# In-place normalization of the next job's rows in the gate and up stage, and the half chunk's split moved from VectorE to GpSimd

## The chip, the cores and the metric

The kernel runs on one core of a Trainium2 chip. The metric is the device time of one execution in microseconds (us); the figure for a kernel is the median of its runs. Every time below comes from those runs or from one profiled execution.

## What is computed

2048 rows of 1024 values (two sequences of 1024) pass three layers, each added to its input: half a feed-forward net, a convolution along the row, and half the same feed-forward net again.

```python
x = x + 0.5 * ffn(layernorm(x))
x = x + attn(layernorm(x))          # a long convolution, its kernel from a state space model
x = x + 0.5 * ffn(layernorm(x))

def layernorm(x): return (x - mean(x)) / sqrt(var(x) + 1e-5)
def ffn(x):       return (silu(x @ Wg) * (x @ Wu)) @ Wd
# Wg, Wu: 1024 x 2752, Wd: 2752 x 1024, each 4 bits with a scale and a zero point per 128 rows
```

## The kernel before

**Jobs.** The rows are cut into four blocks of 512. A job is one block in one of the two feed-forward layers, so there are eight, in the order (block, layer) = (0,1) (1,1) (0,3) (1,3) (2,1) (3,1) (2,3) (3,3); they are called job 0 to job 7. Layer 2, the convolution, has no job of its own: for blocks that left layer 1, its pieces are hung into the gate and up stage of the following job (jobs 1, 2, 5 and 6).

**Two stages in a job.** The *gate and up stage* (`gate_up`, L716) walks 64 steps: eight waves of output chunks, eight groups of 128 input channels in each wave. Waves 0 to 4 (steps 0 to 39) hold six accumulators in PSUM, waves 5 and 6 (steps 40 to 55) four, the last wave (steps 56 to 63) five, the fifth for the *half chunk*: 2752 is 21 chunks of 128 and 64 more, and the last 64 gate and 64 up channels share one accumulator. In each step TensorE (PE in the profile) multiplies every chunk by the low and the high part of the activations (`xTl` in f16, `xTh` in fp32r, L742), and the accumulator is then multiplied in place by the ratio of two groups' scales (`scaled`, L710): on ScalarE (ACT, L712) for the gate chunks, on VectorE (DVE, L714) for the up chunks. The next step's matmul on that accumulator needs the scaled value. At a wave's end `gated` (L767) forms silu(gate) * up: ACT makes the silu `g` (L769), DVE the product `hf` (L772), and GpSimd (POOL) splits it into `hh` (a cast, L774) and `hl` (the rest, L776). `gated_half` (L779) does so for the half chunk, with `hf_half` on DVE (L786) and the split on DVE too:

```python
nc.vector.tensor_copy(both[high], hf[high])                                              # L788
nc.vector.tensor_tensor(both[low], hf[high], both[high].bitcast(F32), ALU.subtract)      # L789
```

The *down stage* (`down`, L794) walks 44 steps, two halves of 22 chunks. A step is eight matmuls (L805), `hl` and `hh` into four accumulators, and four scalings: two on ACT and two on DVE (L714). Chunk 21, the half chunk, is used in step 21 first.

**Weights.** POOL casts the byte weights of a step to fp32r (`make_weights`, L690) three steps before their use; the sync engine's DMA queue (SP) loads the bytes one step before that.

**The next job's activations.** While a job runs, the rows of the next job lie in four tiles `x` of 128x1024. Their moments (L187, L188) and inverse deviations (L210 to L213) are taken in the gate and up stage. For a next job in layer 1 (made in jobs 3 and 4), the moments are written at step 44 and the deviations at step 45. For a next job in layer 3 they follow the convolution, at steps 27 and 28, in job 1 at steps 61 and 62; there the tiles are also saved to DRAM (L1441). From job 1 on, `turn_by_dma` (L253) then does the rest in ten pieces for each of the four tiles t, hung at steps 2+9t and later of the down stage. The first piece normalizes the tile into a new tile `xn`, in two halves on DVE (L269). The next six are POOL's: `hi` and `top` (casts, L276, L277), `mid` (L279) and `lo` (L281), for each half. Then come three DMAs that transpose, and two POOL sums. A job loads its own rows again from DRAM at step 21 of its down stage, for the residual sum.

**What sets the order.** The kernel is written as one program with hooks: a function hung at a step is written ahead of that step's matmuls. A scheduler then orders each engine's instructions, and may put one ahead of others as soon as its inputs are expected to be ready. Where a hook is wrapped in `in_order_of_writing` (L141) with an engine's name, this engine's instructions keep the order in which they were written. Every engine runs its instructions strictly in order. Before the change, the pieces of `turn_by_dma` were so wrapped for POOL and SP, and not for DVE.

Of the kernel before, what the change touches and what calls it, by code (L numbers as in the profile page):

```python
# [9 lines left out]
F32 = mybir.dt.float32  # L10
# [8 lines left out]
ALU = mybir.AluOpType  # L19
AX = mybir.AxisListType  # L20
ET = mybir.EngineType
# [34 lines left out]
def macaron_s4_kernel(  # L56
# [31 lines left out]
    nc = tc.nc  # L88
# [41 lines left out]
    def t4(name):  # L130
        return xpool.tile([P, HID], F32, tag="x", name=name)
# [9 lines left out]
    def in_order_of_writing(f, *engines):  # L141

        start = len(nc.cur_bb.bb.instructions)
        got = f()
        written = list(nc.cur_bb.bb.instructions)
        for e in engines:
            last = next((i for i in reversed(written[:start]) if i.engine == e), None)
            for ins in written[start:]:
                if ins.engine == e:
                    if last is not None:  # L150
                        tc.add_manual_dep(
                            ins,
                            last.name,
                            mybir.DependencyInfo(
                                mybir.DependencyClass.NoSync, mybir.DependencyReason.DATA
                            ),
                            reason="order of writing",
                        )
                    last = ins
        return got  # L160


    x = {}
    ln = {}
# [59 lines left out]
    def turned(n, name):  # L224

        ps = bank(name)
        for k in range(4):
            nc.tensor.transpose(ps[:, bass.ts(k, P)], n[:, bass.ts(k, P)], ident)  # L228
        return ps.rearrange("p (c t) -> p c t", c=4)
# [4 lines left out]
    def turn(b, t, n, half, by_pool=False):  # L234
        k = ln[b, t][2]
        if b not in pieces:
            pieces[b] = [
                xtpool.tile([P, NC, TB], dt, tag=f"xT{w}", name=f"xT{w}_{b}_{k}")
                for w, dt in (("h", F32R), ("l", F16))
            ]  # L240
        hi, lo = (a[:, 4 * half : 4 * half + 4, bass.ts(t, P)] for a in pieces[b])
        ps = turned(n, f"pt_{b}_{k}_{t}_{half}")
        if by_pool:
            both = gpool.tile([P, TB], F32, tag="g", name=f"turn_{b}_{k}_{t}_{half}")
            both = both.rearrange("p (c t) -> p c t", c=4)
            nc.scalar.copy(both, ps)
            nc.gpsimd.tensor_copy(hi, both)
            nc.gpsimd.tensor_tensor(lo, both, hi.bitcast(F32), ALU.subtract)
        else:
            nc.scalar.copy(hi, ps)  # L250
            nc.vector.tensor_tensor(lo, ps, hi.bitcast(F32), ALU.subtract)

    def turn_by_dma(b, t, after):  # L253

        k = ln[b, t][2]
        name = f"{b}_{k}_{t}"
        if b not in pieces:
            pieces[b] = [  # L260
                xtpool.tile([P, NC, TB], dt, tag=f"xT{w}", name=f"xT{w}_{b}_{k}")
                for w, dt in (("h", F32R), ("l", F16))
            ]
        hi_t, lo_t = (a[:, :, bass.ts(t, P)] for a in pieces[b])
        halves = [slice(0, 512), slice(512, HID)]
        m, r, _ = ln[b, t]
        n = t4(f"xn_{name}")
        for own in halves:
            nc.vector.tensor_scalar(n[:, own], x[b][t][:, own], m, r, ALU.subtract, ALU.mult)  # L269
        yield  # L270
        hi = t4(f"hi_{name}").bitcast(F32R)
        top = hfpool.tile([P, HID], BF16, tag="hf", name=f"top_{name}")
        mid = hfpool.tile([P, HID], BF16, tag="hf", name=f"mid_{name}")
        lo = gpool.tile([P, HID], F16, tag="g", name=f"lo_{name}")
        for own in halves:
            nc.gpsimd.tensor_copy(hi[:, own], n[:, own])  # L276
            nc.gpsimd.tensor_copy(top[:, own], n[:, own])  # L277
            yield
            nc.gpsimd.tensor_tensor(mid[:, own], hi[:, own].bitcast(F32), top[:, own], ALU.subtract)  # L279
            yield  # L280
            nc.gpsimd.tensor_tensor(lo[:, own], n[:, own], hi[:, own].bitcast(F32), ALU.subtract)  # L281
            yield
        both = t4(f"turned_{name}").bitcast(BF16).rearrange("p (i c t) -> p i c t", i=2, c=NC)

        def transposes():
            nc.sync.dma_start(both[:, 0], top, transpose=True)
            nc.sync.dma_start(both[:, 1], mid, transpose=True)
            nc.sync.dma_start(lo_t, lo, transpose=True)

        transposes()  # L290

        def sums():
            for half in range(2):
                own = slice(4 * half, 4 * half + 4)
                nc.gpsimd.tensor_tensor(hi_t[:, own], both[:, 0, own], both[:, 1, own], ALU.add)  # L295
                yield

        after.append(sums())
# [273 lines left out]
    def split(w):  # L572
        raw, z = packed[w]
        even = t4(f"even_{w}").bitcast(I32)[:, : width_of(w)]
        return signed_bytes(w, raw, even, z)
# [203 lines left out]
    def gated_half(j, p):  # L779

        last = rat[:, 2 * WIDE, GK - 1 :]
        low, high = slice(0, HALF), slice(HALF, P)
        g = gpool.tile([P, TB], F32, tag="g", name=f"g_{j}_half")
        nc.scalar.activation(g[high], p[low], AF.Silu, scale=last[low])
        hf = hfpool.tile([P, TB], F32, tag="hf", name=f"hf_{j}_half")
        nc.vector.scalar_tensor_tensor(hf[high], p[high], last[high], g[high], ALU.mult, ALU.mult)  # L786
        both = hpool.tile([P, TB], F32R, tag="h", name=f"hb_{j}")
        nc.vector.tensor_copy(both[high], hf[high])  # L788
        nc.vector.tensor_tensor(both[low], hf[high], both[high].bitcast(F32), ALU.subtract)  # L789
        h[WIDE] = (both,)  # L790

    yT = {}

    def down(j, b, hooks):  # L794
# [605 lines left out]
    def fast():  # L1400
        for j, (b, k) in enumerate(JOBS):
            prev = JOBS[j - 1] if j else None
            after = JOBS[j + 1] if j + 1 < len(JOBS) else None
            up, dn = {}, {}

            def at(hooks, s, f):
                hooks.setdefault(s, []).append(f)

            if prev:
# [3 lines left out]
                if pk == 1:  # L1413
                    late = 34 if j == 1 else 0
# [51 lines left out]
            if j == 1:  # L1466
                tables = s4_tables()
                for i in range(S4_PIECES):
                    piece = lambda: in_order_of_writing(lambda: next(tables, None), ET.DVE)
# [3 lines left out]
            if after:  # L1473
                ab, ak = after
                if ak == 1:
                    at(up, 55 if j == 0 else 6, lambda: load_x(ab, rows_of(u, ab)))
                    if j == 0:
                        steps = [(dn, d) for d in range(3, 8)]
                        in_pieces(at, steps, lambda: moments_by_tile(ab, 1))
                        newton = lambda: deviations(ab, 1, LIFT)  # L1480
                        at(dn, 8, lambda: in_order_of_writing(newton, ET.DVE))
                    else:
                        both = lambda: moments(ab, 1)
                        at(up, 44, lambda: in_order_of_writing(both, ET.DVE))
                        at(up, 45, lambda: deviations(ab, 1, LIFT))
                an = {}

                pool = j == 0

                def anorm(t):  # L1490
                    an[t] = normalized(ab, t)

                o = 9 if j == 0 else 0
                turns = {}

                def turning(t):
                    if t not in turns:
                        turns[t] = [], []
                        turns[t] += (turn_by_dma(ab, t, turns[t][1]),)
                    rest = turns[t][1] or turns[t][2:]  # L1500
                    next(rest[0], None)

                for t in range(NT if j else 0):
                    late = (12, 13) if t == NT - 1 else (13, 17)
                    for d in (0, 1, 2, 3, 5, 6, 7, 9) + late:
                        piece = lambda t=t: turning(t)
                        piece = lambda piece=piece: in_order_of_writing(piece, ET.Pool, ET.SP)
                        at(dn, 2 + 9 * t + d, piece)
                for t in range(0 if j else NT):
                    at(dn, o + 1 + 4 * t, lambda t=t: anorm(t))  # L1510
                    at(dn, o + 2 + 4 * t, lambda t=t: turn(ab, t, an[t][:, :512], 0, by_pool=pool))
                    at(dn, o + 4 + 4 * t, lambda t=t: turn(ab, t, an[t][:, 512:], 1, by_pool=pool))
            o, gap = (27, 3) if j == 0 else (21, 4)
            at(dn, o, lambda: load_x(b, rows_of(u, b) if k == 1 else saved(b)))
            for t in range(NT):
# [3 lines left out]
        b = JOBS[-1][0]  # L1519
# [205 lines left out]
```

## Time and profile before

| | |
|---|---|
| median of three runs | 2126.0 us (2123.86 to 2126.82) |
| profiled execution | 2125.47 us |
| its span, first to last instruction | 2123.6 us |
| busy: PE, DVE, ACT, POOL | 98%, 80%, 66%, 61% of the span |
| granted TensorE clock | 0.996 |
| gate and up stage of jobs 2, 3, 7 | 187.4, 159.5, 157.6 us |
| down stage of jobs 2, 3, 7 | 83.8, 83.7 and 94.7 us (the last with the end of the program) |

A job begins about every 240 to 270 us. Job 2's gate and up stage runs from 572.3 to 759.7 us of the span and its down stage from 759.7 to 843.4 us, job 3's from 843.4 and from 1002.9 us; these two jobs are read most below. The timeline prints an instruction's start, its duration, engine, line and tiles, then in brackets the idle time of the engine before it and what ended that. Tile names stand without numbers. Matmuls overlap in the pipeline: in a full stretch one of 512 columns *starts* every 0.225 us in the gate and up stage and every 0.23 us in the down stage, whatever duration is printed, so a stall of PE is read from the distance of two starts.

### The profile page before, as it was taken

What the parts mean: (1) busy time and instruction counts of PE and PEld (TensorE: products, weight loads), DVE (VectorE), ACT (ScalarE), POOL (GpSimd) and SP (SyncE); (2) the same over time, 40 slices, a digit from 0 to 9 for tenths busy, and PEclk for the clock granted to TensorE, in tenths of its full rate; (3) what the DMA queues carried; (4) which work ended last, traced back from release to release, by engine and by line L of the source; (5) the groups of instructions that cost most, each with busy time, mean ns of one, the idle gap of its engine ahead of it and who ended that gap; (6) DMA issues with size and microseconds to landing.
All of it is one profiled execution on the core that took longest, in us unless ns stands there. A gap on an engine that the chain in (4) does not pass through costs nothing.

```text
span 2123.6 us, 30212 instructions
## 1 busy us (share of the span) xinstructions
PE 2071.9 (98%) x9556; PEld 1405.8 (66%) x9556; DVE 1688.6 (80%) x2757; ACT 1396.8 (66%) x2185; POOL 1290.1 (61%) x1678
## 2 busy tenths in 40 slices
PE   6999999999999999999999999999999999999997
PEld 3555675677776567665776567675676766866576
DVE  8988877778888787778877888877788787777776
ACT  5777777736655766676667766547665467667765
POOL 6877838647654577455855568455684546845541
PEclk9999999999999999999999999999999999999999
DMA  4434321113311125211441124111251111441111
GB/s 139 122 86 143 100 72 53 36 54 82 100 39 54 34 58 167 66 30 34 121 135 38 29 50 124 42 53 31 49 123 38 51 39 41 123 128 34 33 35 58
DMA packets 239143, 151.02 MB, mean 71 GB/s; under 512 B 98683, under 2 KB 226532, under 8 KB 238974
## 3 DMA queue, kind: packets, MB, share of 16 engines
q1 hardware_dynamic: 237958, 147.12, 24.6%
q8 instruction: 78, 1.28, 0.3%
q10 hardware_dynamic: 728, 1.29, 0.2%
q14 instruction: 91, 0.75, 0.1%
q0 software_dynamic: 288, 0.59, 0.1%
HBM read 104.45 MB, written 25.50 MB: 61 GB/s over the span
## 4 chain that ended last, share of the span: by engine, by line
PE 88%; DVE 8%; ACT 1%; DMA 1%; issue 1%; POOL 1%; SPq 0%; ACTq 0%; DVEq 0%; POOLq 0%
PE pg L742 56%; PE po L805 26%; PE pc L1131 3%; DVE po L714 2%; PE pb L827 1%; PE pb L1131 1%; DVE pg L714 1%; DVE xn L269 1%; PE st L228 1%; DVE hf L772 0%; DMA b<-wq 0%; DVE rawd L565 0%; POOL q L598 0%; DMA x<-in_L_attn_u_dram 0%; ACT g L769 0%
## 5 line engine op out<-in xcount | busy, mean ns | idle before, releaser
L712 ACT ACTIVATE pg<-pg,rat 128x512 f32<-128x512 f32 x1240 | 786.3, 660 | 423.6 <-PE pg L742 422.5
L714 DVE TENSOR_TENSOR pg<-pg,rat 128x512 f32<-128x512 f32 x1168 | 777.4, 693 | 179.8 <-PE pg L742 175.1
L742 PE MATMUL pg<-xTh,w_up 128*128 128x512 f32 x2752 | 851.0, 438 | 3.0 <-DVE pg L714 1.7
L742 PE MATMUL pg<-xTl,w_up 128*128 128x512 f16 x2752 | 722.0, 382 | 6.2 <-POOL xTl L1580 3.1
L690 POOL CAST w_up<-b 128x768 fp32r<-128x768 int8 (+2 forms) x490 | 376.3, 774 | 504.7 <-PE pg L742 406.6
L742 PEld LDWEIGHTS pg<-xTh,w_up 128*128 128x128 f32 x2752 | 519.7, 189 | 176.9 <-DVE pg L714 14.5
L712 ACT ACTIVATE po<-po,ratd 128x512 f32<-128x512 f32 x660 | 431.2, 661 | 189.9 <-PE po L805 189.8
L805 PE MATMUL po<-hl,w_down 128*128 128x512 f32 x1344 | 535.9, 402 | 14.8 <-DVE po L714 13.2
L805 PE MATMUL po<-hh,w_down 128*128 128x512 f32 x1344 | 521.6, 391 | 0.0
L714 DVE TENSOR_TENSOR po<-po,ratd 128x512 f32<-128x512 f32 x620 | 428.7, 697 | 102.7 <-PE po L805 97.6
L742 PEld LDWEIGHTS <-w_up 128*128 128x128 bf16 x2752 | 228.6, 99 | 330.6 <-issue 155.8
L690 POOL CAST w_down<-bd 128x512 fp32r<-128x512 int8 x352 | 224.3, 639 | 193.1 <-PE po L805 118.8
L805 PEld LDWEIGHTS po<-hl,w_down 128*128 128x128 f32 x1344 | 252.0, 188 | 102.8 <-DVE po L714 40.6
L805 PEld LDWEIGHTS po<-hh,w_down 128*128 128x128 f32 x1344 | 252.6, 188 | 47.0
L776 POOL TENSOR_TENSOR hl<-hf,hh 128x512 fp32r<-128x512 f32 x168 | 217.8, 1297 | 8.1
L772 DVE SCALAR_TENSOR_TENSOR hf<-pg,rat,g 128x512 f32<-128x512 f32 x168 | 123.1, 748 | 48.1 <-ACT g L769 40.8
L769 ACT ACTIVATE g<-pg,rat 128x512 f32<-128x512 f32 x168 | 110.7, 686 | 50.5 <-PE pg L742 34.3
L774 POOL CAST hh<-hf 128x512 fp32r<-128x512 f32 x168 | 105.6, 629 | 58.5 <-PE pg L742 31.0
L281 POOL TENSOR_TENSOR lo<-xn,hi 128x512 f16<-128x512 f32 x48 | 61.7, 1286 | 0.0
L187 DVE BATCH_NORM_STATS2 stats<-x 128x6 f32<-128x512 f32 x88 | 58.5, 676 | 0.5
L279 POOL TENSOR_TENSOR mid<-hi,top 128x512 bf16<-128x512 f32 x48 | 57.0, 1187 | 0.0
L295 POOL TENSOR_TENSOR xTh<-turned 128x512 fp32r<-128x512 bf16 x48 | 55.8, 1163 | 0.0
(214 smaller groups left out, 1116.0 us busy)
## 6 DMA issues: line engine op xcount, KB each, us to landing
b<-wq SPq DMA_DIRECT2D x319, 96.0 KB
bd<-wdq SPq DMA_DIRECT2D x336, 64.0 KB
x<-in_L_attn_u_dram SPq DMA_DIRECT2D x30, 512.0 KB
b<-wq SPq DMA_DIRECT2D x128, 64.0 KB
xs<-x SPq DMA_DIRECT2D x16, 512.0 KB
x<-xs SPq DMA_DIRECT2D x16, 512.0 KB
out_dram<-x SPq DMA_DIRECT2D x16, 512.0 KB
b<-wq SPq DMA_DIRECT2D x64, 80.0 KB
```

The costliest lines, as they stand in the source:

```text
L187: nc.vector.bn_stats(stats[:, t, i, :], x[b][t][:, bass.ts(i, 512)])
L281: nc.gpsimd.tensor_tensor(lo[:, own], n[:, own], hi[:, own].bitcast(F32), ALU.subtract)
L690: nc.gpsimd.tensor_copy(t, b)
L712: nc.scalar.activation(dst, src, AF.Copy, scale=sc)
L714: nc.vector.tensor_tensor(dst, src, sc.to_broadcast([P, TB]), ALU.mult)
L742: nc.tensor.matmul(p, weights, (lo, hi)[k][:, g, :], start=(g == 0 and not done), stop=(g == GK - 1 and done), skip_group_check=True,)
L769: nc.scalar.activation(g, pg, AF.Silu, scale=rat[:, 2 * f, GK - 1 :])
L772: nc.vector.scalar_tensor_tensor(hf, pu, last, g, ALU.mult, ALU.mult)
L774: nc.gpsimd.tensor_copy(hi, hf)
L776: nc.gpsimd.tensor_tensor(lo, hf, hi.bitcast(F32), ALU.subtract)
L805: nc.tensor.matmul(ps[c], w[:, bass.ts(c, P)], part, start=(f == 0 and k == 0), stop=(f == NF - 1), skip_group_check=True,)
L1131: nc.tensor.matmul(dst, lhsT, rhs, start=start, stop=stop, skip_group_check=True)
```

## The change

Three things are changed. The normalization leaves `turn_by_dma`: a new function `normalize` writes it back into `x` itself, half a tile at a time, and the pieces of `turn_by_dma` read `x`; the four `xn` tiles are gone. The eight halves of a job are hung at steps 46, 48, ... 60 of the gate and up stage, in job 1 at steps 0, 1, 3, 4, 6, 7, 9 and 10 of the down stage, and keep the order of writing on DVE. The split of the half chunk becomes two GpSimd instructions, hung at steps 1 and 2 of the down stage in the order of writing on POOL. Job 0, which turns its next rows in another way, has only the last of these.

```diff
+    def normalize(b, t, half):
+        m, r, _ = ln[b, t]
+        part = x[b][t][:, bass.ts(half, 512)]
+        nc.vector.tensor_scalar(part, part, m, r, ALU.subtract, ALU.mult)
+
     def turn_by_dma(b, t, after):
...
-        m, r, _ = ln[b, t]
-        n = t4(f"xn_{name}")
-        for own in halves:
-            nc.vector.tensor_scalar(n[:, own], x[b][t][:, own], m, r, ALU.subtract, ALU.mult)
-        yield
+        n = x[b][t]
...
-        nc.vector.tensor_copy(both[high], hf[high])
-        nc.vector.tensor_tensor(both[low], hf[high], both[high].bitcast(F32), ALU.subtract)
         h[WIDE] = (both,)
+        def split():
+            nc.gpsimd.tensor_copy(both[high], hf[high])
+            yield
+            nc.gpsimd.tensor_tensor(both[low], hf[high], both[high].bitcast(F32), ALU.subtract)
+        half_split[j] = split()
...
                 for t in range(NT if j else 0):
                     late = (12, 13) if t == NT - 1 else (13, 17)
-                    for d in (0, 1, 2, 3, 5, 6, 7, 9) + late:
+                    for half in range(2):
+                        piece = lambda t=t, half=half: normalize(ab, t, half)
+                        piece = lambda piece=piece: in_order_of_writing(piece, ET.DVE)
+                        at(*((dn, 3 * t + half) if j == 1 else (up, 46 + 4 * t + 2 * half)), piece)
+                    for d in (1, 2, 3, 5, 6, 7, 9) + late:
                         piece = lambda t=t: turning(t)
                         piece = lambda piece=piece: in_order_of_writing(piece, ET.Pool, ET.SP)
                         at(dn, 2 + 9 * t + d, piece)
...
+            for d in (1, 2):
+                piece = lambda j=j: next(half_split[j], None)
+                at(dn, d, lambda piece=piece: in_order_of_writing(piece, ET.Pool))
```

More of the change, by code (lines that the diff above doesn't have):

```diff
@@ L787, in gated_half @@
         both = hpool.tile([P, TB], F32R, tag="h", name=f"hb_{j}")
-        nc.vector.tensor_copy(both[high], hf[high])
-        nc.vector.tensor_tensor(both[low], hf[high], both[high].bitcast(F32), ALU.subtract)
         h[WIDE] = (both,)
+        def split():
[3 more added lines that the diff above has]
+        half_split[j] = split()
+    half_split = {}
     yT = {}
```

## The prediction

> **What bounds the kernel now.** I read the page first, the chain of work that ended last.
>
> ```profile
> PE 88%; DVE 8%; ACT 1%; DMA 1%; issue 1%; POOL 1%; SPq 0%; ACTq 0%; DVEq 0%; POOLq 0%
> ```
>
> PE sets the end; DVE stands in the chain for 8%. So only an edit that lets PE wait less, or more, for DVE can matter. The waits say where, and the groups what the moved instruction costs:
>
> ```profile
> PEld po L805 <- DVE po L714: 40.6, 80, 1.6
> PE po L805 <- DVE po L714: 13.2, 25, 1.2
> L269 DVE TENSOR_SCALAR xn<-x,mv,r 128x512 f32<-128x512 f32 x48 | 39.7, 827 | 0.1
> ```
>
> PE (and its weight loads) waits in the down stage for a DVE scaling. That a normalization stands before the late scaling is seen in the timelines of job 2's down stage: DVE, POOL, PE.
>
> ```profile
> 773.30 0.70 DVE L714 TENSOR_TENSOR po<-po,ratd 128x512 f32<-128x512 f32 x1 [0.21 <-PE po L805]
> 773.91 0.54 DVE L269 TENSOR_SCALAR xn<-x,mv,r 128x512 f32<-128x512 f32 x1
> 774.37 0.69 DVE L714 TENSOR_TENSOR po<-po,ratd 128x512 f32<-128x512 f32 x1
> 774.97 1.37 DVE L269 TENSOR_SCALAR xn<-x,mv,r 128x512 f32<-128x512 f32 x1
> 776.26 1.28 DVE L714 TENSOR_TENSOR po<-po,ratd 128x512 f32<-128x512 f32 x2
> ```
> ```profile
> 774.89 1.16 POOL L279 TENSOR_TENSOR mid<-hi,top 128x512 bf16<-128x512 f32 x1
> ```
> ```profile
> 776.05 0.39 PE L805 MATMUL po<-hh,w_down 128*128 128x512 f32 x1
> 777.00 0.50 PE L805 MATMUL po<-hl,w_down 128*128 128x512 f32 x1 [0.56 <-DVE po L714]
> 777.34 0.40 PE L805 MATMUL po<-hh,w_down 128*128 128x512 f32 x1
> ```
>
> Undisturbed, the scaling after 773.30 would start 0.91 later, at 774.21; after the first normalization it starts 0.16 late. The second takes 1.37, because POOL's `mid` runs until 776.05: it ends 0.29 after that. The next scaling starts at 776.26 in place of 775.12, 1.14 late, and PE starts at 777.00, 0.95 after its last matmul in place of 0.23: a stall of 0.72, and 0.11 more on the next. 1.14 - 0.72 = 0.42 was slack. This pairing of scalings with the matmuls that need them, done for every bank by the written order, gives the usable slack (distance from a scaling's end to that matmul, less the 0.06 that stalled ones show): 0.40 in the down stage, **only 0.17 in waves 5 and 6** of the gate and up stage, 0.38 to 0.62 in the last wave for the scalings that will follow a normalization, none for the first scaling of wave 6.
>
> **Part 1, normalizations out of the down stage (gain).** In the built order of before, tile 0's two halves of jobs 2 to 6 already stand in the gate and up stage: the scheduler had drawn them there. So six of eight leave each of these five down stages. They stall PE three times there, in job 2 at 777.00 and 794.21 (0.72 + 0.11 each) and at 812.38 (0.16 + 0.11): 1.93 a job. Nothing else is late at those places, so 5 x 1.93 = **9.7 gained**.
>
> **Part 2, half chunk to POOL (gain).** The start of job 2's down stage on DVE:
>
> ```profile
> 761.98 0.70 DVE L714 TENSOR_TENSOR po<-po,ratd 128x512 f32<-128x512 f32 x1
> 762.71 0.67 DVE L788 CAST hb<-hf_half 64x512 fp32r<-64x512 f32 x1
> 763.41 0.70 DVE L714 TENSOR_TENSOR po<-po,ratd 128x512 f32<-128x512 f32 x1
> 764.14 0.92 DVE L789 TENSOR_TENSOR hb<-hf_half,hb 64x512 fp32r<-64x512 f32 x1
> 765.09 1.30 DVE L714 TENSOR_TENSOR po<-po,ratd 128x512 f32<-128x512 f32 x2
> ```
>
> PE stalls at 764.16 (0.37 + 0.11) and 765.85 (0.20 + 0.11). Without the cast the second scaling ends at about 763.3, ahead of the matmul due at 763.8; without the subtraction the third starts when PE frees its bank. So 0.79 a job, in jobs 2 to 7: **4.7 gained**. In job 0, DVE is busy without a pause from 198.7 to 218, and two stalls there (1.27 and 1.33) wait for it. The split took 1.3 of this; I take **0.8**, between 0, should POOL (busy from 194 to 208) become late instead, and 1.3.
>
> On POOL, no 64x512 form is in the trace. By the rows of 128x512 (L774 cast 0.61, L776 subtraction 1.28) it adds 1.9 a job; bounds: 0.45 (the 128x128 sum, L1128) + 0.6 below, 0.8 + 1.8 (the longest met at job 0's start) above. In the built order it stands behind `hl` of chunk 20, between casts of w_down. The cast for step 5 ends at 765.1 and is needed at about 769; 1.9 or even 2.6 later it is still early, and POOL's first idle 0.98 (before 772.43) takes half of the delay back. The half chunk itself is needed 20 steps later. Cost 0; if the weights were late after all, up to 1 a job.
>
> **Part 3, normalizations in the gate and up stage (cost).** All that do not meet a POOL instruction cost 0.54 there: the ten that before has in that stage last 0.53 to 0.55, and the next scaling starts 0.45 to 0.48 after theirs. In jobs 2, 5 and 6 the built order puts them behind these: the 6th scaling pair of wave 5; `hf` of chunk 16; the 2nd, 4th and 6th pair of wave 6; `hf` of chunk 18; and twice pg_42 in the last wave. DVE idles 0.2 ahead of each scaling in waves 5 and 6. A single one makes the next scaling 0.16 late, under the 0.17: no stall. Three do cost. Behind `hf` of chunk 16:
>
> ```profile
> 727.77 0.75 DVE L772 SCALAR_TENSOR_TENSOR hf<-pg,rat,g 128x512 f32<-128x512 f32 x1 [0.18 <-ACT g L769]
> 728.43 1.29 DVE L714 TENSOR_TENSOR pg<-pg,rat 128x512 f32<-128x512 f32 x2
> ```
> ```profile
> 728.55 1.27 POOL L776 TENSOR_TENSOR hl<-hf,hh 128x512 fp32r<-128x512 f32 x1
> 730.89 1.29 POOL L776 TENSOR_TENSOR hl<-hf,hh 128x512 fp32r<-128x512 f32 x1
> ```
>
> The scaling at 728.43 has no slack, so a normalization ahead of it stalls PE by 0.46. It would start 0.12 before `hl`. At 420.82 a normalization with that lead lasted 0.80, its plain time for 1024 columns, and `hl` 1.83: DVE went first. The next one, two pairs on, falls into the second `hl`, which the first pushed on to end at about 732.75: to 733.04, next scaling 0.66 late, stall 0.49. Behind `hf` of chunk 18, slack 0.29: stall 0.17. With 0.1 of refill behind each, 1.4 a job, 3 x 1.4 = **4.2 lost**. Jobs 3 and 4 have the moments at step 44, and DVE works that off until about 981 in job 3. Behind it the built order now holds four normalizations in a row (before: one at 980.94, one at 982.60). The next scaling comes 3 x 0.46 later, by about 1.5 with a cast of w_up met; slack 0.26; stall 1.25. With those at the wave's end, 1.9 a job: **3.8 lost**. Bounds per job: 0.5 if PE's reordered matmuls of these jobs hide it, 4 if each `hl` goes first.
>
> [...] By `hl` first at every wave end, the sum would be that of the third rival.
>
> **Part 4, job 1.** Its deviations come at step 62, so the eight stay in the down stage, now spread over steps 0 to 10, where POOL's two-input work is dense. Before, this stage stalls at 491.63, 494.52, 505.74, 522.95 and 541.10: 3.08 in all. The last three (1.9) go. The first two stay: a normalization stands now ahead of the first scaling, meets `hl` of chunk 19 and makes 0.64 into about 0.95. Of the other six I let two or three meet POOL: 0.9. Net **0.5 gained**, between +1.9 and -1. In place, DVE must also wait until the tiles' saves have been read; they are issued by 478.3, and the first overwriting comes at about 490: nothing. The loads at step 21 find their tiles' earlier users at the same steps as before.
>
> **Sum.** 9.7 + 4.7 + 0.8 + 0.5 - 4.2 - 3.8 = 7.7. The profiled execution took 2125.47 (span 2123.6), so **2117.8**; the median, 2126.0, lies 0.5 above, so I say 2118. The measurement tells some 0.2% from no change: faster is under 2121.75, slower over 2130.25.
>
> **The rivals.**
> - *The gate and up stage hides the move.* The reordered matmuls of jobs 3 and 4 leave 0.7 a job, and the wave ends 0.5: cost 2.9. 15.7 - 2.9: 2112.7. For it: DVE idles over 0.2 in every 0.9 there. Against: 0.17 of slack. Chance 0.24.
> - *Forecast*, 2115 to 2121.5: 0.46.
> - *`hl` goes first at the wave ends.* The normalization behind `hf` then lasts until 0.29 after 729.82, which is 1.68 in place of 0.54: 1.15 more at two places in jobs 2, 5 and 6 (6.9), and I take 1.75 for each of jobs 3 and 4 (3.5). The row at 602.54 (1.70) shows it for 1024 columns. Together 2128.2 if always, 2122 to 2126 if in half of them. Or POOL's split makes weights late, 4.7 lost: 2122.5, where the half split would not do what it is for. Chance 0.21.
> - *The stage that takes them is worse than the one that gave them* (slower). If two halves there behave as a pair of the down stage, one of them met by POOL, a pair stalls 0.72 + 0.23 for the smaller slack + 0.11 = 1.06; four pairs in five jobs: 21.2 - 15.7, so 2131. It decides from one in two normalizations met by a POOL instruction. Against: ten of ten rows there show 0.53 to 0.55. Chance 0.09.
>
> The range that holds eight in ten reaches from the first rival's low end, 2111, into the third, to 2127. Faster 0.70, same 0.21, slower 0.09.
>
> **What would show it.** Right: no DVE normalization in the down stages of jobs 2 to 6, these 2 us shorter (and 0.8 by the split); waits of PE on L714 in the down stage down from 54 us (40.6 + 13.2) to some 40; normalizations of 0.54 in the gate and up stage. Wrong: many of 1.2 or more there; the gate and up stages of jobs 2 to 6 longer by over 2; PE waiting for w_down in steps 5 to 9.

## The result, and the profile after

The changed kernel takes **2116.1 us** (median of 7 runs, 2111.99 to 2120.81), against 2126.0 (7 runs, 2122.55 to 2126.94) for the kernel before in the same session: ratio 0.9957, interval 0.9944 to 0.9969. So it is faster by 9.9 us, and the forecast was 2118. The execution that was profiled is the slowest of the seven, 2120.81 (span 2118.6), which has to be kept in mind below. Line numbers have moved by a little: the scalings are L714 (ACT) and L716 (DVE) now, the matmuls L744 and L813, and the normalization is L257.

A stage's length is counted from its first matmul to the first of the next stage. With the experiments e1 (only the normalizations moved), e2 (only the split moved), e3 and e6, which are told below (the 22 us ahead of job 0 and job 7's gate and up stage, 157.1 to 157.7 in all of them, are left out):

| stage (us) | before | after | e1 | e2 | e3 | e6 |
|---|---|---|---|---|---|---|
| job 0, gate and up | 175.9 | 180.4 | 176.6 | 178.3 | 177.1 | 176.1 |
| job 0, down | 96.7 | **101.7** | 95.7 | **100.2** | 95.8 | 97.2 |
| job 1, gate and up | 193.3 | 193.3 | 191.4 | 192.9 | 192.9 | 192.9 |
| job 1, down | 84.3 | 82.2 | 84.8 | 83.6 | 82.2 | 82.3 |
| jobs 2 to 6, gate and up, sum | 880.1 | 884.6 | 885.3 | 879.8 | 884.1 | 880.2 |
| jobs 2 to 6, down, sum | 419.0 | 402.9 | 408.0 | 413.3 | 402.8 | 403.0 |
| job 7, down and end | 94.7 | 93.6 | 94.8 | 93.7 | 94.2 | 94.0 |
| span | 2123.6 | 2118.6 | 2116.5 | 2121.2 | 2108.3 | 2106.0 |

Jobs 1 to 7 are 14.6 us shorter in the profile after (1814.3 against 1828.9). Job 0 is 9.5 *longer*: 4.5 in its gate and up stage, 5.0 in its down stage. The sum came out near the forecast, but its parts did not. One of e3's six executions took 2338.45 us at a granted clock of 0.835 (the other five 0.996 to 0.998), and its ratio below leaves that one out.

In the changed kernel's page, the chain that ended last has DVE at 5% where it had 8%; in the waits, PE's waits for a scaling in the down stage are 27.4 us (19.0 + 8.4) where they were 53.8; those in the gate and up stage are as before (13.9 + 3.0 against 14.5 + 2.8), although that stage of jobs 2 to 6 grew by 4.5. What it lost is read from the distances of PE's starts, below.

```profile
PE 90%; DVE 5%; POOL 2%; issue 1%; ACT 1%; DMA 1%; SPq 0%; DVEq 0%; POOLq 0%; ACTq 0%
```
```profile
PEld po L813 <- DVE po L716: 19.0, 34, 2.5
PEld pg L744 <- DVE pg L716: 13.9, 45, 0.9
PE po L813 <- DVE po L716: 8.4, 8, 2.1
PE pg L744 <- DVE pg L716: 3.0, 10, 0.5
```

The start of job 2's down stage, DVE and then POOL, shows the split gone from the one and standing on the other. DVE now waits for PE ahead of its scalings (the 0.23 in brackets), where before PE waited for DVE:

```profile
770.28 1.30 DVE L716 TENSOR_TENSOR po<-po,ratd 128x512 f32<-128x512 f32 x2
771.81 2.22 DVE L716 TENSOR_TENSOR po<-po,ratd 128x512 f32<-128x512 f32 x3 [0.23 <-PE po L813]
774.26 0.70 DVE L716 TENSOR_TENSOR po<-po,ratd 128x512 f32<-128x512 f32 x1 [0.23 <-PE po L813]
```
```profile
772.85 0.61 POOL L793 CAST hb<-hf_half 64x512 fp32r<-64x512 f32 x1
...
774.22 1.29 POOL L795 TENSOR_TENSOR hb<-hf_half,hb 64x512 fp32r<-64x512 f32 x1
```

The split takes 0.61 + 1.29 = 1.9 on POOL, as estimated from the rows with twice the partitions (0.61 and 1.28): half the partitions did not shorten it.

**Where the moved normalizations cost.** The end of job 2's wave 5: DVE, POOL, PE.

```profile
735.93 0.54 DVE L257 TENSOR_SCALAR x<-x,mv,r 128x512 f32<-128x512 f32 x1
736.38 2.09 DVE L716 TENSOR_TENSOR pg<-pg,rat 128x512 f32<-128x512 f32 x3
738.71 0.70 DVE L716 TENSOR_TENSOR pg<-pg,rat 128x512 f32<-128x512 f32 x1 [0.24 <-PE pg L744]
739.31 0.93 DVE L257 TENSOR_SCALAR x<-x,mv,r 128x512 f32<-128x512 f32 x1
```
```profile
736.04 1.55 POOL L778 TENSOR_TENSOR hl<-hf,hh 128x512 fp32r<-128x512 f32 x1
...
738.67 1.28 POOL L778 TENSOR_TENSOR hl<-hf,hh 128x512 fp32r<-128x512 f32 x1
```
```profile
737.12 0.38 PE L744 MATMUL pg<-xTl,w_up 128*128 128x512 f16 x1 [0.21 <-DVE pg L716]
...
740.90 0.38 PE L744 MATMUL pg<-xTl,w_up 128*128 128x512 f16 x1 [0.21 <-DVE pg L716]
```

The one behind `hf` of chunk 16 starts 0.11 ahead of `hl`, keeps its 0.54, and `hl` takes 1.55: DVE goes first, as forecast. The next falls into the second `hl` (738.67 to 739.95) and ends 0.29 after it. By the distances of PE's starts, 737.12 is late by 0.42 more than the same matmul before the change, 740.90 by 0.36, and one behind `hf` of chunk 18 (752.35) by 0.15. The steps had 0.46, 0.49 and 0.17, with 0.1 of refill behind each. There was hardly any: the four starts from 737.12 take 0.94 and the five from 740.90 take 1.14, where 0.225 each gives 0.90 and 1.13. The stage grew by 0.8, not 1.4.

**Job 0.** Its gate and up stage has its instructions in the same order as before; it took 175.8 to 180.4 in the ten profiles of this study (e2 and e4, whose job 0 has the order of the changed kernel on every engine in both stages, took 178.3 and 175.8). In the profile after, PE stood idle for 2.34 ahead of 177.31, for a cast of w_up at 176.53 for which POOL had waited 4.86 for the DMA (before the change 2.85, at 174.14), and the granted clock fell, to 0.64 in the 4.5 us from 177.0 (the columns are the stretch, its length, busy time and instructions of PE, of its weight loads, DVE, ACT and POOL, then the clock, the DMA share and GB/s):

```profile
174.00:177.00 3.00, 0.97 (x5) 0.34 (x3) 2.38 (x5) 0.47 (x2) 0.47 (x1) 0.97 0.45 126
177.00:181.50 4.50, 4.19 (x13) 1.85 (x14) 1.26 (x2) 3.29 (x6) 2.48 (x5) 0.64 0.50 149
181.50:186.00 4.50, 4.50 (x22) 2.75 (x21) 3.35 (x6) 4.00 (x8) 3.61 (x6) 1.00 0.39 113
```

(The clock is the third number from the end: 0.97, 0.64, 1.00.) That part of job 0's loss belongs to this execution and not to the change. Its down stage is another matter. DVE at its start, in the changed kernel:

```profile
204.12 0.76 DVE L788 SCALAR_TENSOR_TENSOR hf_half<-pg,rat,g_half 64x512 f32<-64x512 f32 x1
204.91 0.85 DVE L567 TENSOR_SCALAR rawd<-rawd 88x512 int32<-88x512 int32 x1
205.79 0.70 DVE L716 TENSOR_TENSOR po<-po,ratd 128x512 f32<-128x512 f32 x1
206.40 1.74 DVE L569 TENSOR_TENSOR rawd<-rawd,zd 88x1024 uint16<-88x1024 uint16 x1
208.06 0.83 DVE L567 TENSOR_SCALAR rawd<-rawd 88x512 int32<-88x512 int32 x1
208.81 0.82 DVE L571 TENSOR_SCALAR rawd<-rawd 88x1024 uint16<-88x1024 uint16 x1
209.56 1.28 DVE L716 TENSOR_TENSOR po<-po,ratd 128x512 f32<-128x512 f32 x2
```

`rawd` are the zero-point pieces of w_down, which job 0 alone has. With the split gone from DVE, the scheduler has put them in its place: one ahead of the first scaling and three between the first and the second. The second, which begins 3.77 after the first, makes PE wait 2.09 (its matmul at 210.29). A second wait of that size comes at 265.13. There a piece of `rawd` that takes 0.79 in e3 (at 254.75) takes 2.58, beside three POOL instructions in a row that end at 264.19, and the scaling behind it is late. DVE, then PE at both places:

```profile
261.29 0.68 DVE L716 TENSOR_TENSOR po<-po,ratd 128x512 f32<-128x512 f32 x1
261.89 2.58 DVE L571 TENSOR_SCALAR rawd<-rawd 88x1024 uint16<-88x1024 uint16 x1
264.39 1.28 DVE L716 TENSOR_TENSOR po<-po,ratd 128x512 f32<-128x512 f32 x2
```
```profile
210.29 0.50 PE L813 MATMUL po<-hl,w_down 128*128 128x512 f32 x1 [2.09 <-DVE po L716]
...
265.13 0.50 PE L813 MATMUL po<-hl,w_down 128*128 128x512 f32 x1 [1.90 <-DVE po L716]
```

Behind both waits the granted clock fell again, to 0.62 and 0.58 (first PE alone, then all engines, in the columns given above):

```profile
207.50:210.20 2.70, 0.70 (x4) 1.00 0.00 0
210.20:213.20 3.00, 2.90 (x8) 0.62 0.14 42
213.20:216.00 2.80, 2.70 (x9) 0.80 0.28 74
```
```profile
265.00:268.50 3.50, 3.37 (x11) 2.74 (x12) 1.37 (x3) 1.32 (x2) 3.50 (x6) 0.58 0.28 80
```

By these figures the first fall took at most 3.0 x 0.38 + 2.8 x 0.20 = 1.7 from PE and the second 3.5 x 0.42 = 1.5 in the stretch shown. In the kernel before, the clock is 1.00 over job 0's whole down stage (198.0 to 294.0), so up to 3.2 of the 5.0 lost there are the clock's.

### The profile page after: what moved, and what is told of

Same layout as the page of the kernel before. It is cut to its first block, busy times and chain, and to the rows that moved or that the text cites. A ratio compares the mean times of both kernels' runs of the same rounds, so it can differ in the third digit from the quotient of the medians.

```text
span 2118.6 us, 30223 instructions
## 1 busy us (share of the span) xinstructions
PE 2065.1 (97%) x9556; PEld 1410.2 (67%) x9556; DVE 1674.5 (79%) x2741; ACT 1398.4 (66%) x2185; POOL 1298.0 (61%) x1694
## 3 DMA queue, kind: packets, MB, share of 16 engines
q8 instruction: 78, 1.28, 0.3%
q10 hardware_dynamic: 728, 1.29, 0.2%
## 4 chain that ended last, share of the span: by engine, by line
PE 90%; DVE 5%; POOL 2%; issue 1%; ACT 1%; DMA 1%; SPq 0%; DVEq 0%; POOLq 0%; ACTq 0%
PE pg L744 54%; PE po L813 28%; PE pc L1139 3%; DVE pg L716 2%; PE pb L835 1%; PE pb L1139 1%; PE st L228 1%; DVE po L716 0%; POOL q L600 0%; DMA b<-wq 0%; DVE x L257 0%; ACT pg L714 0%; DVE rawd L571 0%; DVE rawd L569 0%; DVE hf L774 0%
## 5 line engine op out<-in xcount | busy, mean ns | idle before, releaser
L714 ACT ACTIVATE pg<-pg,rat 128x512 f32<-128x512 f32 x1240 | 786.7, 660 | 431.2 <-PE pg L744 429.8
L716 DVE TENSOR_TENSOR pg<-pg,rat 128x512 f32<-128x512 f32 x1168 | 775.8, 693 | 171.6 <-PE pg L744 166.4
L744 PE MATMUL pg<-xTh,w_up 128*128 128x512 f32 x2752 | 855.9, 438 | 4.7 <-DVE pg L716 1.9
L744 PE MATMUL pg<-xTl,w_up 128*128 128x512 f16 x2752 | 725.7, 382 | 11.7 <-POOL w_up L692 5.5
L744 PEld LDWEIGHTS pg<-xTh,w_up 128*128 128x128 f32 x2752 | 519.4, 189 | 181.3 <-DVE pg L716 13.9
L714 ACT ACTIVATE po<-po,ratd 128x512 f32<-128x512 f32 x660 | 432.4, 661 | 176.0 <-PE po L813 175.6
L813 PE MATMUL po<-hl,w_down 128*128 128x512 f32 x1344 | 534.0, 399 | 9.0 <-DVE po L716 8.4
L716 DVE TENSOR_TENSOR po<-po,ratd 128x512 f32<-128x512 f32 x620 | 430.3, 698 | 119.2 <-PE po L813 115.0
L813 PE MATMUL po<-hh,w_down 128*128 128x512 f32 x1344 | 523.5, 392 | 0.0
L744 PEld LDWEIGHTS <-w_up 128*128 128x128 bf16 x2752 | 228.2, 99 | 336.9 <-issue 158.9
L692 POOL CAST w_down<-bd 128x512 fp32r<-128x512 int8 x352 | 217.5, 620 | 171.9 <-PE po L813 96.5
L813 PEld LDWEIGHTS po<-hl,w_down 128*128 128x128 f32 x1344 | 252.6, 188 | 80.0 <-DVE po L716 19.0
L813 PEld LDWEIGHTS po<-hh,w_down 128*128 128x128 f32 x1344 | 253.6, 189 | 49.4
L283 POOL TENSOR_TENSOR lo<-x,hi 128x512 f16<-128x512 f32 x48 | 62.0, 1291 | 0.0
```

What stands on the lines that cost most here:

```text
L692: nc.gpsimd.tensor_copy(t, b)
L714: nc.scalar.activation(dst, src, AF.Copy, scale=sc)
L716: nc.vector.tensor_tensor(dst, src, sc.to_broadcast([P, TB]), ALU.mult)
L744: nc.tensor.matmul(p, weights, (lo, hi)[k][:, g, :], start=(g == 0 and not done), stop=(g == GK - 1 and done), skip_group_check=True,)
L813: nc.tensor.matmul(ps[c], w[:, bass.ts(c, P)], part, start=(f == 0 and k == 0), stop=(f == NF - 1), skip_group_check=True,)
```

## Experiments

All were timed against the kernel before, in the same session on the same chip. Theory A, formed on reading this: the split on POOL costs job 0 about 5, through DVE's order. Its rival B: job 0 was longer by chance. The first four ran together (before: 2125.91).

**e1_norms_only: the split back on DVE.**

```diff
-        def split():
-            nc.gpsimd.tensor_copy(both[high], hf[high])
-            yield
-            nc.gpsimd.tensor_tensor(both[low], hf[high], both[high].bitcast(F32), ALU.subtract)
+        nc.vector.tensor_copy(both[high], hf[high])
+        nc.vector.tensor_tensor(both[low], hf[high], both[high].bitcast(F32), ALU.subtract)
... (and the hooks of the two pieces at steps 1 and 2 are gone)
```

> The changed kernel with the half chunk split on DVE again, in all jobs; the normalizations stay moved and in place. Theory A (in job 0 the split on POOL left DVE's order open to long zero-point work ahead of the down stage's scalings, which cost about 4.8 of the median): job 0 gets that back, jobs 1 to 7 lose the split's 0.79 each (5.5), so 2116.1 - 4.8 + 5.5 = 2116.8. Rival B (job 0 was longer in the profiled execution by chance of its DMA landings, and the change has no part in it): only the 5.5 are lost, 2121.6. Under both, job 2's down stage is some 0.8 longer than the 80.6 of the changed kernel, and its gate and up stage the same 188.2.

Measured: 2120.05, ratio 0.9974 (0.9963 to 0.9985). By the time alone it stands between the two theories; by the stages job 0's down stage is back (95.7), and jobs 1 to 7 lose 7.7 against the changed kernel, not 5.5. In this profile job 1's gate and up stage, which the edit does not touch, is 1.9 shorter than in the changed kernel (see the last section); without it they lose 9.5. So A for job 0, with the split in the other jobs worth more than I had put on it. The down stages of jobs 2 to 6 are 11.0 shorter than before by the moved normalizations alone.

**e2_split_only: the kernel before, with the same split on POOL.** (The edit of e1 turned round, in the kernel before.)

> The kernel before with the split of the half chunk on POOL, normalizations as before. Theory A: jobs 1 to 7 gain 5.5, job 0 loses 4.8: 2125.3, no difference that can be measured. Rival B: 2120.5. Under both, the down stages of jobs 2 to 6 are some 0.8 shorter than 83.8.

Measured: 2123.33, ratio 0.9987 (0.9978 to 0.9996), a small gain, and a time between A's 2125.3 and B's 2120.5. Job 0's down stage is 100.2, near the 101.7 of the changed kernel, with the same two waits (208.25 and 261.63). Jobs 1 to 7 gain 8.5. The sum of the two parts, 6.9 (e1) + 8.5 = 15.4, is near the 14.6 with both only by luck: without job 1's gate and up stage it is 5.0 + 8.2 = 13.2 against 14.7, and the difference lies in job 1's down stage.

**e3_job0_dve: the changed kernel, the split on DVE in job 0 alone.**

```diff
+        if j == 0:
+            nc.vector.tensor_copy(both[high], hf[high])
+            nc.vector.tensor_tensor(both[low], hf[high], both[high].bitcast(F32), ALU.subtract)
+            return
... (and job 0 has no hooks for the two pieces)
```

> The changed kernel, with the split of the half chunk on DVE in job 0 alone. Theory A: job 0 gets its 4.8 back and nothing else moves: 2111.3, and job 0's down stage is about 97 us, not 101.7. Rival B: 2116 with a scatter of 4 us, job 0's down stage as long as that of e2.

Measured: 2110.15, ratio 0.9927 (0.9914 to 0.9940), job 0's down stage 95.8: near A's 2111.3, and B falls. DVE at the same place:

```profile
201.34 0.87 DVE L793 CAST hb<-hf_half 64x512 fp32r<-64x512 f32 x1
202.25 0.70 DVE L716 TENSOR_TENSOR po<-po,ratd 128x512 f32<-128x512 f32 x1
202.98 1.62 DVE L794 TENSOR_TENSOR hb<-hf_half,hb 64x512 fp32r<-64x512 f32 x1
204.62 0.72 DVE L567 TENSOR_SCALAR rawd<-rawd 88x512 int32<-88x512 int32 x1
205.27 0.68 DVE L716 TENSOR_TENSOR po<-po,ratd 128x512 f32<-128x512 f32 x1
```

The split itself takes 2.5 of DVE here, but the second scaling begins 3.02 after the first, where it was 3.77: taking the split away made it later.

**e4_in_place_down: in place, hung in the down stage.**

```diff
-                    for half in range(2):
-                        piece = lambda t=t, half=half: normalize(ab, t, half)
-                        piece = lambda piece=piece: in_order_of_writing(piece, ET.DVE)
-                        at(*((dn, 3 * t + half) if j == 1 else (up, 46 + 4 * t + 2 * half)), piece)
+                    at(dn, 2 + 9 * t, lambda t=t: [normalize(ab, t, half) for half in range(2)])
```

> The changed kernel, but with both halves of a tile hung at the step of the down stage where they stood before (2+9t) and no order of writing on DVE. In the built order the scheduler then draws all eight of jobs 2, 5 and 6 into waves 3 and 4 of the gate and up stage and those of jobs 3 and 4 into waves 6 and 7; job 1's eight stay in the down stage, one ahead of each second scaling. Theory A (what gains is that no normalization stands in the down stage, and writing in place is enough for that): as the changed kernel or a little better, 2112 to 2117, with the gate and up stages of jobs 2, 5, 6 back at 187.4 and 186.4. Rival C (the written steps 46 to 60 matter): slower than the changed kernel by 2 us or more.

Measured: 2117.59, ratio 0.9965 (0.9952 to 0.9977). That is 0.6 above A's range and 0.5 short of C's, and the interval overlaps that of the changed kernel (0.9944 to 0.9969), so the time does not decide; the down stages of jobs 2 to 6 have their 80.6. So the scheduler moves those of jobs 2 to 6 by itself when they write in place. But the gate and up stages of jobs 2, 5 and 6 are 188.5, 187.5 and 187.4, not the 187.4 and 186.4 expected: waves 3 and 4 are no free place either. There too some fall into an `hl`, as in job 5, DVE and POOL:

```profile
1447.59 1.28 DVE L257 TENSOR_SCALAR x<-x,mv,r 128x512 f32<-128x512 f32 x1
```
```profile
1447.32 1.27 POOL L778 TENSOR_TENSOR hl<-hf,hh 128x512 fp32r<-128x512 f32 x1
```

The next three ran together (before: 2126.41). e5 asks whether A's mechanism is DVE's order, or POOL being late in job 0 (D); e6 whether the cost in the gate and up stage is that of single places (E) or of the DVE time as such (F); e7 whether writing in place matters (G) or the place in the order alone (H).

**e5_job0_later: the split on POOL everywhere, job 0's six zero-point pieces one or two steps later.**

```diff
                 steps = [when(max(0, n - d)) for d in (4, 3, 3, 2, 1, 0)]
+                if k == 2:
+                    steps = [(dn, d) for d in (1, 2, 2, 3, 3, 4)]
```

> The changed kernel, split on POOL in job 0 too; only the six zero-point pieces of the third part of w_down (rawd_2, DVE), which job 0 had at steps 0, 0, 0, 1, 2 and 3 of its down stage, are hung at steps 1, 2, 2, 3, 3 and 4. In the built order the first scaling then stands right behind hf_half, and never more than two of these pieces between two scalings; POOL's order is not touched. Theory A (DVE's order): job 0's down stage goes from about 101 to 96 us, the time to 2110 to 2112. Rival D (POOL's two more instructions make its later work late in job 0): job 0 stays at about 101 us, 2115 to 2117.

Measured: 2109.16, ratio 0.9918 (0.9905 to 0.9932); job 0's down stage 93.4, the shortest of all and 3.3 below the kernel before. The time is just below A's range. POOL still has its two more instructions, so D falls. The wait of 2.09 is gone by DVE's order, as A says: the first two scalings come ahead, while POOL's order up to there is that of the changed kernel.

```profile
203.42 0.70 DVE L718 TENSOR_TENSOR po<-po,ratd 128x512 f32<-128x512 f32 x1
204.15 0.88 DVE L567 TENSOR_SCALAR rawd<-rawd 88x512 int32<-88x512 int32 x1
204.95 1.28 DVE L718 TENSOR_TENSOR po<-po,ratd 128x512 f32<-128x512 f32 x2
```

For the wait at 265.13, A is not shown. DVE's order there is the same in both kernels, but the `rawd` piece takes 0.79 here (at 254.89). Against the expectation, POOL's order *was* touched further on: copies of `rawd` from 213.40 in the profile after, and casts, copies and `xTl` work between 238 and 259, stand in other places, and so do some instructions of PE (from 206.95 here) and ACT. Which of these removed that wait is open. What the runs do show is that job 0's down stage goes with its built order as a whole. The kernel before, e1, e3, e6 and e7 have one order in job 0, the same on every engine, and take 95.7 to 97.2; the changed kernel, e2 and e4 share another and take 100.2 to 101.8; e5 and e8 share a third and take 93.4 and 93.5.

**e6_spread: other places for the normalizations** (job 0 as in e3).

```diff
-                        at(*((dn, 3 * t + half) if j == 1 else (up, 46 + 4 * t + 2 * half)), piece)
+                        steps = (52, 54, 57, 58, 59, 60, 61, 62) if ak == 1 else (42, 44, 46, 52, 54, 58, 60, 62)
+                        at(*((dn, 1 + 3 * t + half) if j == 1 else (up, steps[2 * t + half])), piece)
```

> Split on DVE in job 0 as in e3_job0_dve (2110.15), and other steps for the normalizations: jobs 2, 5 and 6 at 42, 44, 46, 52, 54, 58, 60, 62 (none behind hf of chunk 16 or 18, none beside hl of a wave's end), jobs 3 and 4 at 52, 54, 57 to 62 (so none in a row behind the deviations), job 1 one step later in the down stage (not ahead of the first scaling). Theory E (the places cost, one by one: 0.8, 0.5, 0.5 in jobs 2, 5, 6, about 1 in each of jobs 3 and 4, 1.1 in job 1): these go, 2110.15 - 4.5 = about 2105.7. Rival F (what costs is the DVE time itself, 8 x 0.46 a job, wherever it stands in that stage): 2109 to 2111.

Measured: 2106.19, ratio 0.9906 (0.9891 to 0.9921). E: the gate and up stages of jobs 2 to 6 sum to 880.2, within 0.1 of the kernel before, which has two halves there where this one has eight. Six normalizations more, 6 x 0.46 = 2.8 of DVE time a job, cost nothing in the right places, even where an `hl` met two of them (in job 4, 1.05 at 1224.68 and 0.95 at 1227.45). One thing is not separated from the places: in these stages PE's matmuls, which the change had reordered, most of all in jobs 3 and 4, stand in the order of the kernel before again. The one miss is job 1, still 82.3. Its first normalization now starts only 0.03 ahead of an `hl`, where 0.11 was enough at 735.93, and loses: 1.60, to 0.28 after `hl`'s end.

```profile
492.44 1.60 DVE L257 TENSOR_SCALAR x<-x,mv,r 128x512 f32<-128x512 f32 x1
```
```profile
492.47 1.29 POOL L778 TENSOR_TENSOR hl<-hf,hh 128x512 fp32r<-128x512 f32 x1
```

**e7_moved_to_xn: moved, but into new tiles** (job 0 as in e3).

```diff
-        part = x[b][t][:, bass.ts(half, 512)]
-        nc.vector.tensor_scalar(part, part, m, r, ALU.subtract, ALU.mult)
+        if half == 0:
+            xn[b, t] = t4(f"xn_{b}_{t}")
+        own = bass.ts(half, 512)
+        nc.vector.tensor_scalar(xn[b, t][:, own], x[b][t][:, own], m, r, ALU.subtract, ALU.mult)
...
-        n = x[b][t]
+        n = xn.pop((b, t))
```

> As e3_job0_dve (2110.15), but the moved normalizations write a new tile xn as before the change, four tiles a job, not x itself; the order of every engine is that of e3. Theory G (in place matters: the fourth xn tiles must wait for buffers that are free only in the down stage, and DVE, which runs in order, waits with them, with the scalings queued behind): slower than e3, by 3 us or more. Rival H (place alone matters, there are buffers enough): 2110.

Measured: 2110.48, ratio 0.9929 (0.9916 to 0.9943), e3's time (2110.15). H: no buffer is missing when the kernel runs, and with the order written out, in place or not makes no difference. Why the scheduler left six of eight in the down stage before the change, and none in e4, is a matter of its plan and stays open.

**e8_best: the pieces of e5 and e6 together**, with job 1's normalizations at steps 2, 4, 5, 6, 7, 8, 10 and 11. (A later session; before: 2125.53.)

> The pieces of e5_job0_later (split on POOL in every job, six zero-point pieces of job 0 a step later) and e6_spread (the places in the gate and up stages) in one kernel, and job 1's normalizations at steps 2, 4, 5, 6, 7, 8, 10, 11 of the down stage, so that the first issues after the last hl of the wave's end has ended. If the terms add up: 2106.19 (e6) less the 1.0 by which e5 is below e3 (2110.15 - 2109.16), and less up to 0.9 for job 1's stall of 0.87 that e6 still shows in its down stage: 2104.3 to 2105.2. Rival F again (some of the DVE time comes back elsewhere, job 1's POOL work waits for the later first half): 2106 or more.

Measured: **2102.78**, ratio 0.9898 (0.9882 to 0.9915), the fastest of all, 22.8 below the kernel before. The terms add up for job 0 (down stage 93.5) and for the gate and up stages of jobs 2 to 6 (880.1). The time is 1.5 below the expected 2104.3, but not for the reason given: job 1's down stage stays at 82.3, because a later normalization (at 500.83, 1.32 long) now meets POOL and stalls PE by 0.52. In the profiles e8 is 4.9 shorter than e6. Of this, 3.7 are in job 0's down stage, for which 1.0 was expected (it was the difference of two medians), and 1.4 in job 1's gate and up stage, 191.4 against 192.9, which the edit does not touch (see the last section); the rest nearly cancels.

## Why the prediction was right, and where it was not

The sign and the size were right: 9.9 gained where 8 was forecast. That is partly luck. Jobs 1 to 7 gained 14.6 where the steps gave 6.9, and job 0's down stage lost 5.0 where they gave 0.8 gained: 14.6 - 5.0 = 9.6, close to the 9.9 of the medians. Two errors of opposite sign nearly met.

- **Part 1** (9.7 gained): 11.0, by e1. The mechanism is as told: the stalls at 777.00, 794.21 and 812.38 and their like are gone. Of the 0.27 a job that was missed, 0.1 is the refill at 811.52; the rest stays open. The sign named for it, waits of PE falling from 54 to some 40, came out stronger (27.4): one stall stands in that view twice, at the weight loads (0.98 at 777.00) and at PE (0.56), and the forecast took it off once.
- **Part 2, jobs 2 to 7** (4.7 gained): 5.8, by e3 against e1. In e2, without the moved normalizations, it is 6.8: there the stall of 0.72 in job 2 became 0.19 and 0.28, since POOL's `mid` and the normalization now met otherwise. On POOL it costs 1.9, as forecast. That no 64x512 form was in the trace is a misreading: the kernel before has four two-input instructions of 64x512 on POOL (L921 and L923, 1286 and 1272 ns on average), from which the 1.29 could have been read.
- **Part 2, job 0** (0.8 gained, between 0 and 1.3): **this step failed.** I let two waits shrink by the 1.3 that the split takes on DVE, and looked for harm on POOL only. What happened is that the scheduler filled the freed time with longer work. The built order in job 0 had changed, and I priced the old one. By the distances of PE's starts, one stall of 2.26 (210.29) stands in place of the 1.27 and the 1.33, one of 2.06 is new (265.13), and the granted clock fell behind each. The forecast had no such fall, and it is up to 3.2 of the 5.0. The loss is 5.0 to 5.9 by the stage's length (101.7 against 96.7 and, in e3, 95.8) and 6.0 by the medians (2116.1 against 2110.15). e2 to e5 show job 0's built order to be its cause; that it is DVE's order is shown for the first wait only.
- **Part 3** (8.0 lost): 4.5 in the profile after, 5.2 in e1. The three places in jobs 2, 5 and 6 were named rightly and each was some 10 to 40% too dear; of the refills of 0.1 at most 0.04 came behind 737.12 and 740.90; and jobs 5 and 6, whose matmuls were reordered there, lost 0.4 and 0.5. Jobs 3 and 4, with the burst of four, lost 1.9 and 0.9, not 1.9 twice; before the change these two stages had differed by 1.0 already, and after it they are equal. e6 takes the whole of it back by other places; how much of that is PE's order, which came back with them, is not shown.
- **Part 4** (0.5 gained, without the split): job 1's down stage gained 2.1 with both parts. Alone, the moved normalizations lose 0.5 there (e1) and the split gains 0.7 (e2); the two help each other, which a sum of parts could not show. The stall ahead of the first scaling is there (1.02), with a normalization of 1.00 for the 0.95 forecast.
- **The rivals.** That the gate and up stage hides the move was nearer than my forecast for that stage (4.5, between its 2.9 and my 8.0). That `hl` goes first at the wave ends did not come: at 735.93 DVE went first, with a lead of 0.11. In e6 the same pairing did come, once, at a lead of 0.03. By the starts that the trace records, leads of 0.10 and 0.11 were enough for DVE, 0.03 and 0.08 were not (last section); what decides between the two engines is not shown beyond these rows. The slower rival needed one in two normalizations met by POOL; it was two in eight in jobs 2, 5 and 6, and two of eight in jobs 3 and 4.

What stays open is how much of job 0's gate and up stage (175.8 to 180.4) is chance of the DMA landings alone: no run changed them.

## What to carry to other kernels

When work leaves an engine whose order a scheduler sets, read what the scheduler puts in its place, instruction by instruction: here the split taken from DVE made a scaling later, and moving six small pieces by one or two steps won that back (6.9 us of the median). Here a short instruction on DVE, which was idle for 20% of the span, was free or cost its full length by its place: in the places of e6 eight cost nothing; ahead of a scaling without slack, or inside two-input work of POOL, one cost 0.15 (752.35 after the change) to 0.83 (777.00 before it). And a total that agrees with the forecast proves no step of it; only stage by stage did the two errors show.

## What the runs showed of the hardware

- In the profile after, PE stood idle for 2.34, 2.09 and 1.90 us ahead of 177.31, 210.29 and 265.13, and the granted clock was then 0.64 in the 4.5 us from 177.0, 0.62 in the 3.0 from 210.2 and 0.58 in the 3.5 from 265.0. It is 0.50 in one stretch of 3.41 us each time (176.79 to 180.21, 210.93 to 214.34 and 265.54 to 268.95), so each of these falls cost at most 1.7. After the stalls of 1.27 and 1.33 (idle for 1.10 and 1.16) in the kernel before it stayed at 1.00 (204.3 to 207.0 and 207.7 to 210.5). But the length of the stall did not decide alone. In the profile after, PE was also idle for 3.16 and 2.45 ahead of 48.60 and 55.52, and the clock stayed at 1.00 (48.6 to 55.5 and 55.5 to 60.0). e2 has the same order in job 0 and the same wait of 2.09 at 208.25, and its clock stayed at 1.00 (208.2 to 212.0): behind the wait, the same matmul came after 2.51 (210.76) in e2 and after 3.92 (214.21) in the changed kernel, 1.4 later. In e2 the clock fell at 241.83 instead, behind a wait of only 1.15 (240.10).
- In job 1's gate and up stage a stretch of narrow matmuls (`s_sums`, 128x8, for the convolution's tables) ends near 365. The clock after it was 0.60 for 3.9 us in the kernel before and 1.00 in e1 and e8. That stage is 191.4 or 191.5 in e1, e7 and e8, whose clock is 1.00 from 360 to 380, and 192.9 to 193.3 in the other seven profiles, whose clock is 0.91 there: 1.5 us of scatter that go with the clock. Why it falls in some executions and not in others no edit here explains.
- A cast (201.34 in e3) and two normalizations on DVE (739.31 after the change, 492.44 in e6) that lost to a POOL instruction ended 0.28 or 0.29 after it, at lengths of 0.87, 0.93 and 1.60. One piece lost to several in a row: that of `rawd` at 261.89 after the change took 2.58 and ended 0.28 after the third. A recorded lead of 0.10 (495.17 in e6) or 0.11 was enough to win, one of 0.03 (492.44 in e6) or 0.08 (988.59 in e4, 1.64 long) was not.
- Two-input work on DVE was stretched beside POOL as well: the 88x1024 piece that takes 0.67 at 205.87 in e3 took 1.74 beside `hl` at 206.40 after the change.
